# Four graph layers on one core: layer 1's projection by seven block products, its matrix divided before use, and its scores placed between layer 2's products

## The chip, the cores and the metric

The kernel runs on one core of a Trainium2 chip. The time is device microseconds of one launch, the median over several runs. The engines are named as in the profile: PE (TensorE, matrix products; PEld are its weight loads), DVE (VectorE), ACT (ScalarE), POOL (GpSimd) and SP (SyncE, whose queue issues nearly all DMA transfers here). Each engine works through its own list of instructions in order and waits on semaphores for the others.

## The reference, cut to what matters

`x` is 128 graphs of 64 nodes with 512 features, `adj` is 128 matrices of 64 x 64. Four layers follow each other, each wrapped as `x = layernorm(x + layer(x))`, all in float32. The change is in layer 1 and in the order of the steps around it:

```python
def _L1_gnn_ref(x, A_shape, w, a):
    y = x @ w
    s = y @ a
    A = s[..., :, None] + s[..., None, :]
    A = jnp.tanh(A / 8.0) * 8.0
    A = jnp.where(A >= 0, A, 0.1 * A)
    A = jnp.exp(A) * A_shape
    A = A / jnp.sum(A, axis=-1, keepdims=True)
    A = A * jnp.sum(A_shape, axis=-1, keepdims=True)
    return A @ x @ w
```

Layer 0 is a hypergraph convolution with a hidden width of 1024 (products with W1 and W2), layer 2 three graph convolutions (products with W1, W2, W3), layer 3 an attention with eight heads (products with the q, k and v parts of `W_qkv`, and with `W_out`), a mask and a bias.

## The kernel before

**Tiles.** The 8192 rows are cut into 16 groups of 512 rows: four pairs of graphs, 128 rows each. A group's state `xg` is a tile of 128 partitions x 4 pairs x 512 features in a pool of three buffers (`xp`), so the x load of a group waits until the store of the group three before it has landed. Features are brought to the partitions by `graph_T` (L341), which at the same time multiplies each graph by its 64 x 64 matrix: 64 small matmuls (128 passes in the trace) for each half of the pairs, copied out of PSUM by ACT into a `Left` (L367), the left side of a large product.

**Large products by seven.** All large products but layer 1's go through `multiply` (L409). It cuts left, right and result into 2 x 2 blocks and forms seven block products in place of eight, in the order B11, T1, T2, B21, T3, B22, T4. `product` (L391) issues one of them: four 128x256 matmuls, which float32 makes eight passes in the trace. The four sums of left blocks that this needs are made on DVE by `Left.sums` (L377). Of the weights, three blocks come from the input; the four differences T1 to T4 are formed once, in group 0, by `Weight.make` (L197), written to DRAM, and loaded from there for later groups. Three partial results are taken out of PSUM in the middle by `snap` (L414; ACT copies, or DVE adds where a residual is added) and added to later ones on DVE (L434, L436, L438). `multiply` is a generator: it yields once, after the third product, so that other work can be placed in its middle. Its accumulators `a`, `b`, `c` are the names of its PSUM tiles; with the key they make names such as `a_q` (first accumulator of the q product) or `c_wo`.

**Weights.** The class `Stream` (L244) walks a list of uses in the order of the schedule and issues weight loads on SP's queue, as long as at most 20 tiles of 256 KB are held (`RING`). Layer 1's `w` is a special case there: `None` in place of a `Weight`, four tiles of 128 rows x 512.

**Layer 1** is the end of `first_half` (L543). `s4` holds the scores of the rows (L611), `e` spreads them on a diagonal (L615), a matmul with `bones` (ones on two 64 x 64 blocks) gives `ss` (L619), and on it follow an add, Tanh, the leaky part, and Exp (L624 to L627). Then `tn = t * adn` (L630) has rows summed (L633) for a reciprocal `r` of each node's denominator, scaled by the row sums of `adj` (L635), and `t = t * atc` (L631) is the undivided matrix, transposed. `graph_T` applies it (step c3), and 16 matmuls of 512 columns (32 passes), in four PSUM tiles, multiply by `w` (L645). DVE multiplies each result by `r` and adds the residual in one instruction (L648); `layer_norm` (L328) ends the layer.

**Order.** The work of a group is in two generators: `first_half` (layers 0 and 1) and `second_half` (layers 2 and 3). A list written out by hand, `order` (L875), gives a step of the whole kernel: `a.` entries advance the first half of group s, `b.` the second half of group s-1, and `t.` the late part of the second half (from the v product on) of group s-2. 18 steps run it: step 0 has only `a`, steps 1 to 15 have an `a` part beside the others, 16 and 17 none. The list sets priorities. A planner then places every instruction on its engine's list when the kernel is built, by its own estimate of the times, so that work further down the list can stand ahead of an instruction that it expects to wait: in the trace a block product of `wo` stands among those of l2c although the list has it behind them. `tc.issue_after` (used by `behind`, L364) puts instructions behind a given one on its engine: behind the last DVE add of a product (`last_add`, L438).

**Layer 3's end.** `wo` is the product with `W_out`; it adds the residual `xg`, to which the bias `bo_bc` was added on DVE in step xT (L744). Then come the last norm and the store on SP's queue (L778), all within step `o`.

Of the kernel before, what the change touches and what calls it, by code (L numbers as in the profile page):

```python
# [20 lines left out]
T = G * P  # L21
KD = D // P
# [18 lines left out]
def kernel(  # L41
# [198 lines left out]
    w_g = [Weight(t, 0, f"gw{'abc'[n]}") for n, t in enumerate((gW1, gW2, gW3))]  # L240
    w_q, w_k, w_v = (Weight(Wqkv, n * D, f"w{'qkv'[n]}") for n in range(3))
    w_o = Weight(Wout, 0, "wo")

    class Stream:  # L244


        def __init__(self, uses):
            self.todo = []
            for wt, q in uses:
                if wt is None:  # L250
                    self.todo.append((wt, q, None, KD))
                elif q == 0:
                    self.todo.append((wt, q, None, 8 * wt.halves))
                else:
                    self.todo += [(wt, q, what, wt.halves) for what in ORDER]
            self.here = {}
            self.held = 0

        def pump(self):
            while self.todo and self.held + self.todo[0][3] <= RING:  # L260
                wt, q, what, n = self.todo.pop(0)
                if wt is None:
                    got = []
                    for c in range(KD):
                        t = wring.tile([P, D], FP, name=f"ww_{q}_{c}", tag="wq")
                        nc.sync.dma_start(out=t, in_=w[c * P : (c + 1) * P, :])
                        got.append(t)
                elif q == 0:
# [6 lines left out]
        def take(self, wt, q, what=None):  # L275
            self.pump()
            if wt is None:
                return self.here.pop((wt, q, None))
# [6 lines left out]
        def done(self, wt, q, what=None):  # L285

            if wt is None:
                self.held -= KD
            elif q > 0:
# [74 lines left out]
    def behind(key):  # L364
        return tc.issue_after(last_add[key]) if key in last_add else nullcontext()
# [40 lines left out]
                )  # L406
        stream.done(*wt_q, what)

    def multiply(lefts, wt_q, dst, key, flipped=False, res=None, before=None):  # L409


        acc = [ps_acc.tile([P, 2, Q], FP, name=f"{n}_{key}", tag="acc") for n in "ab"]
# [1 line left out]
        def snap(ps, m, n, what):  # L414
            t = work.tile([P, 2, Q], FP, name=f"{what}_{key}", tag="w")
            if res is None:
                nc.scalar.copy(t, ps)
            else:
                nc.vector.tensor_add(t, ps, res(m, n))  # L419
            return t  # L420
# [3 lines left out]
        if before is not None:  # L424
            before()
        s1 = snap(pa, 0, 0, "u1")
        product(pc, lefts, wt_q, T1, True, False, flipped)
        s5 = snap(pc, 1, 1, "u5")
        product(pa, lefts, wt_q, T2, False, False, flipped)
        s2 = snap(pa, 0, 1, "u2")  # L430
        yield
        pb = ps_acc.tile([P, 2, Q], FP, name=f"c_{key}", tag="acc")
        product(pb, lefts, wt_q, B21, True, True, flipped)
        nc.vector.tensor_add(dst(0, 0), pb, s1)  # L434
        product(pa, lefts, wt_q, T3, False, False, flipped)
        nc.vector.tensor_add(dst(1, 1), pa, s5)  # L436
        product(pc, lefts, wt_q, B22, False, True, flipped)
        last_add[key] = nc.vector.tensor_add(dst(0, 1), pc, s2).ins  # L438
        product(pa, lefts, wt_q, T4, False, True, flipped)
# [9 lines left out]
    def nat(t):  # L449

        return lambda m, n: t[:, 2 * m : 2 * m + 2, n * Q : (n + 1) * Q]
# [91 lines left out]
    def first_half(g):  # L543
# [90 lines left out]
        nc.vector.reciprocal(r, r)  # L634
# [6 lines left out]
        ww = stream.take(None, q)  # L641
        for p in range(G):
            ps = ps_acc.tile([P, D], FP, name=f"l1w_{q}_{p}", tag="acc")
            for c in range(KD):
                nc.tensor.matmul(  # L645
                    ps, left.t[:, c, p * P : (p + 1) * P], ww[c], start=(c == 0), stop=(c == KD - 1)
                )
            nc.vector.scalar_tensor_tensor(xg[:, p, :], ps, r[:, p : p + 1], xg[:, p, :], ALU.mult, ALU.add)  # L648
            if p == 1:
                yield "p1"  # L650
        stream.done(None, q)
        layer_norm(xg, f"l1_{q}")
        yield "p2"

# [6 lines left out]
    def second_half(g):  # L661
# [82 lines left out]
        nc.vector.tensor_add(xg, xg, bo_bc.unsqueeze(1).to_broadcast([P, G, D]))  # L744
# [33 lines left out]
        nc.sync.dma_start(  # L778
            out=out[q * T : (q + 1) * T, :].rearrange("(p t) d -> t p d", t=P), in_=xg
        )  # L780
        yield "o"

    def scores(g, duo, qT, kT):

# [66 lines left out]
    def attend(g, duo, pts, v, left):  # L851
# [29 lines left out]
    used = {  # L881
        "a.w1a": w_1[0], "a.w1b": w_1[1], "a.w2": w_2, "a.p2": None, "b.l2a": w_g[0], "b.l2b": w_g[1],
        "b.l2c": w_g[2], "b.q": w_q, "b.k": w_k, "t.v": w_v, "t.o": w_o,
    }
    lag = {"a": 0, "b": 1, "t": 2}
# [81 lines left out]
```

## Time and profile before

| | before |
|---|---|
| median of 4 runs | 2866.37 us (2865.38 to 2867.57) |
| the profiled execution's own time | 2865.38 us |
| its span, first to last instruction | 2863.6 us |
| mean granted PE clock | 0.992 |
| layer 1's product, PE busy (L645) | 229.2 us, 512 passes of 596 ns, overlapping |
| a block product's first form (`a_q`), PE busy | 85.3 us, 360 passes of 380 ns, overlapping |
| weight load of layer 1 (`ww`) | 64 transfers of 256 KB, 2.8 us to land |
| x load, store of the result | 6.0 us and 4.3 us to land (1024 KB each) |

How to read it: times are in microseconds, the mean of one instruction in ns. Matmul passes are pipelined, so the durations of passes that follow each other overlap; what a run of them takes is read from start to start in the timeline. A wait is listed by who waited and for what, with total, times and longest. The chain of waits follows back from the last instruction to what released it at each step; with a window it shows the part of the chain in that stretch. A row with a line number of a helper (L402 in `product`, L333 in `layer_norm`) covers all its callers, so tiles' names tell them apart.

### The profile page before, as it was taken

The numbers are of one execution on the slowest core, as the hardware profiler recorded it, in microseconds if no ns is written. First come the engines' busy times: TensorE is split into PE (matmuls) and PEld (weight loads), VectorE is DVE, ScalarE is ACT, GpSimd is POOL, SyncE is SP. The second block draws the span as 40 slices with busy tenths as digits, with TensorE's granted clock in tenths as the row PEclk, the third lists the DMA queues.
The fourth block names the chain that finished last, engine by engine and source line by source line (L and its number), as shares of the span: only waits on it lengthen the run. The fifth ranks groups of instructions, "written<-read, shape, count | busy, mean of one in ns | idle before, by whom it ended". The sixth has DMA issues, their size and how long they took to land.

```text
span 2863.6 us, 66482 instructions
## 1 busy us (share of the span) xinstructions
PE 2793.3 (98%) x28386; PEld 2284.6 (80%) x28386; DVE 1955.9 (68%) x3849; ACT 774.8 (27%) x1380; POOL 7.8 (0%) x17
## 2 busy tenths in 40 slices
PE   6899999999999999999999999999999999999998
PEld 4687878878788787887878788787887878888776
DVE  6667776667665766766667666776767677666655
ACT  2122322223222232322223222232232323122232
POOL 1000000000000000000000000000000000000000
PEclk9899999999999999999999999999999999999999
DMA  6444445444444445444444444444444444344431
GB/s 190 144 134 130 132 127 162 130 150 127 154 134 132 143 129 161 128 129 152 130 154 127 131 154 131 149 127 157 132 125 150 132 155 128 119 158 130 134 118 60
DMA packets 300294, 393.14 MB, mean 137 GB/s; under 512 B 57152, under 2 KB 172128, under 8 KB 300000
## 3 DMA queue, kind: packets, MB, share of 16 engines
q1 hardware_dynamic: 299344, 387.28, 43.6%
q8 instruction: 225, 3.69, 0.5%
q0 software_dynamic: 656, 1.60, 0.2%
q14 instruction: 69, 0.57, 0.1%
HBM read 358.90 MB, written 29.88 MB: 136 GB/s over the span
## 4 chain that ended last, share of the span: by engine, by line
PE 81%; DVE 14%; DMA 2%; ACT 2%; issue 1%; SPq 0%; DVEq 0%; ACTq 0%
PE a_l0w L402 15%; PE b_l0w L402 7%; PE a_l2b L402 4%; PE c_l0w L402 4%; PE a_l2a L402 4%; PE a_l2c L402 4%; PE a_k L402 4%; PE a_v L402 4%; DVE st_l L333 4%; PE a_q L402 3%; PE gt_l L351 3%; PE gt_l0h L351 2%; PE a_wo L402 2%; PE b_l2a L402 2%; PE b_v L402 2%; PE b_k L402 2%
## 5 line engine op out<-in xcount | busy, mean ns | idle before, releaser
L645 PE MATMUL l1w<-ww,aT_l 128*128 128x512 f32 x512 | 229.2, 596 | 0.0
L645 PEld LDWEIGHTS l1w<-ww,aT_l 128*128 128x128 f32 x512 | 96.1, 190 | 104.5 <-issue 97.6
L333 DVE BATCH_NORM_STATS2 st_l<-x 128x6 f32<-128x512 f32 x256 | 168.2, 679 | 1.7
L324 ACT ACTIVATE rs_l<-mv_l,eps_t 128x4 f32<-128x4 f32 x64 | 19.0, 297 | 546.7 <-DVE mv_l L334 546.7
L402 PE MATMUL a_l0w<-w2w,aT_l0h 128*128 128x256 f32 x720 | 164.3, 381 | 0.0
L402 PEld LDWEIGHTS a_l0w<-w2w,aT_l0h 128*128 128x128 f32 x720 | 135.6, 190 | 18.8
L568 ACT ACTIVATE h<-h 128x1024 f32<-128x1024 f32 x64 | 67.6, 1057 | 264.8 <-DVE h L438 241.4
L337 DVE TENSOR_SCALAR x<-x,mv_l,rs_l 128x512 f32<-128x512 f32 x256 | 122.1, 541 | 1.2
L359 ACT COPY aT_l<-gt_l 128x512 f32<-128x512 f32 x192 | 99.0, 599 | 58.0 <-PE gt_l L351 58.0
L402 PE MATMUL b_l0w<-w2w,s_l0h 128*128 128x256 f32 x480 | 108.5, 379 | 0.0
L402 PEld LDWEIGHTS b_l0w<-w2w,s_l0h 128*128 128x128 f32 x480 | 91.2, 190 | 12.4
L402 PE MATMUL a_l2b<-gwbw,aT_h 128*128 128x256 f32 x360 | 86.9, 384 | 4.7 <-ACT aT_oT L871 4.7
L703 ACT ACTIVATE aT_h<-gth,gb_col 128x256 f32<-128x256 f32 x128 | 48.4, 489 | 159.0 <-PE gth L695 159.0
L402 PE MATMUL a_l0w<-w1aw,aT_l 128*128 128x256 f32 x360 | 88.2, 388 | 0.0
L419 DVE TENSOR_TENSOR u_l0w<-a_l0w,b_bc 128x512 f32<-128x512 f32 x64 | 44.0, 687 | 64.4 <-PE a_l0w L402 64.4
L402 PE MATMUL a_l2c<-gwcw,aT_h 128*128 128x256 f32 x360 | 87.7, 386 | 0.0
L402 PE MATMUL a_l2a<-aT_l,gwaw 128*128 128x256 f32 x360 | 86.6, 383 | 1.0 <-ACT aT_l L359 1.0
L402 PE MATMUL a_l0w<-w1bw,aT_l 128*128 128x256 f32 x360 | 87.3, 379 | 0.0
L402 PE MATMUL a_v<-wvw,aT_xT 128*128 128x256 f32 x360 | 86.6, 383 | 0.0
L402 PE MATMUL a_wo<-wow,aT_oT 128*128 128x256 f32 x360 | 86.0, 382 | 0.2 <-DVE x L436 0.2
L507 DVE TENSOR_TENSOR smat<-sps,rb 64x256 f32<-64x256 f32 x32 | 13.5, 422 | 105.4 <-PE sps L504 104.9
L402 PE MATMUL a_q<-aT_xT,wqw 128*128 128x256 f32 x360 | 85.3, 380 | 0.2 <-ACT aT_xT L742 0.2
(427 smaller groups left out, 6119.9 us busy)
## 6 DMA issues: line engine op xcount, KB each, us to landing
w2w<-w2k SPq DMA_DIRECT2D x210, 256.0 KB, 2.6
x<-in_x_dram SPq DMA_DIRECT2D x16, 1024.0 KB, 6.0
ww<-in_w_dram SPq DMA_DIRECT2D x64, 256.0 KB, 2.8
out_dram<-x SPq DMA_DIRECT2D x16, 1024.0 KB, 4.3
w1aw<-w1ak SPq DMA_DIRECT2D x60, 256.0 KB, 2.7
w1bw<-w1bk SPq DMA_DIRECT2D x60, 256.0 KB, 2.6
gwaw<-gwak SPq DMA_DIRECT2D x60, 256.0 KB, 2.6
gwbw<-gwbk SPq DMA_DIRECT2D x60, 256.0 KB, 2.6
```

Source lines behind the costliest of these rows:

```text
L324: nc.scalar.activation(rs, mv[:, :, 1], AF.Sqrt, bias=eps_t)
L333: nc.vector.bn_stats(st, xg[:, p, :])
L337: nc.vector.tensor_scalar(xg[:, p, :], xg[:, p, :], mv[:, p, 0:1], rs[:, p : p + 1], ALU.subtract, ALU.mult)
L351: nc.tensor.matmul(ps[g][f * C : (f + 1) * C, c, p, :], src(2 * duo + p)[rows, c0 : c0 + C], mat[rows, 2 * duo + p, :], start=True, stop=True,
L359: nc.scalar.copy(o[:, :, :, g, :], ps[g])
L402: nc.tensor.matmul(acc[:, blk, :], lhsT, rhs, start=(first and blk == 0 and i == 0), stop=(last and i == n_k - 1), skip_group_check=True,)
L419: nc.vector.tensor_add(t, ps, res(m, n))
L507: nc.vector.tensor_mul(sm[rows], s_ps[h][rows], rb[rows])
L568: nc.scalar.activation(hn, hn, AF.Relu)
L645: nc.tensor.matmul(ps, left.t[:, c, p * P : (p + 1) * P], ww[c], start=(c == 0), stop=(c == KD - 1))
L703: nc.scalar.activation(o[:, :, h, :], ps[h][:, c].rearrange("p (d a) i -> p d (a i)", d=2), AF.Relu, bias=gb2_col[:, k : k + 1],)
```

## The change

- Layer 1's `w` becomes a `Weight` (`w_l1`), and its projection goes through `multiply`: seven loads for a group in place of four, four differences made and stored in group 0, left sums on DVE, a result tile `y` in SBUF. The special case leaves `Stream`.
- The matrix is divided before it is applied: `t` is multiplied by `atc` at once, a matmul with `bones` gives the column sums `den` of the transposed matrix in PSUM, DVE takes their reciprocal (`rd`, 128 x 256) and multiplies. `tn`, `r` and the reduction are gone. The last multiply-add takes `y` and the row sums of `adj`.
- `multiply` gets `stops`, the block products after which it yields. l2c yields after the third and the fifth, `ss` stands between the fifth and the end. `wo` yields after the first and the third, and `den` stands between these.
- The bias add of layer 3 moves from step xT behind the last add of the q product. The last norm and the store become a step of their own, `ln3`, behind `b.q`, issued behind the last add of the next group's q product.

```diff
+    w_l1 = Weight(w, 0, "w")
...
-    def multiply(lefts, wt_q, dst, key, flipped=False, res=None, before=None):
+    def multiply(lefts, wt_q, dst, key, flipped=False, res=None, before=None, stops=(3,)):
...
         s1 = snap(pa, 0, 0, "u1")
+        if 1 in stops:
+            yield
         product(pc, lefts, wt_q, T1, True, False, flipped)
...
         s2 = snap(pa, 0, 1, "u2")
-        yield
+        if 3 in stops:
+            yield
...
         nc.vector.tensor_add(dst(1, 1), pa, s5)
+        if 5 in stops:
+            yield
...
         nc.scalar.activation(t, t, AF.Exp, scale=8.0)
-
-        tn = grp.tile([P, G, C], FP, name=f"tn_{q}", tag="tn", bufs=1)
-        nc.vector.tensor_mul(tn, t, g["adn"])
         nc.vector.tensor_mul(t, t, g["atc"])
-        r = small.tile([P, G], FP, name=f"r_{q}", tag="r")
-        nc.vector.reduce_sum(r, tn, axis=AX.X)
-        nc.vector.reciprocal(r, r)
-        nc.vector.tensor_mul(r, r, g["rowsum"])
         yield "ss"
+
+        den = ps_gt.tile([P, G, C], FP, name=f"den_{q}", tag="gt")
+        nc.tensor.matmul(
+            den.rearrange("p a i -> p (a i)"), bones.rearrange("p g j -> p (g j)"),
+            t.rearrange("p a i -> p (a i)"), start=True, stop=True,
+        )
+        rd = grp.tile([P, G, C], FP, name=f"rd_{q}", tag="rd", bufs=1)
+        nc.vector.reciprocal(rd, den)
+        nc.vector.tensor_mul(t, t, rd)
+        yield "den"
         left = Left(f"l1_{q}")
         for duo in range(2):
             graph_T(pair, t, left.t, duo, f"l1_{q}")
+        left.sums()
         yield "c3"
...
+        y = big.tile([P, G, D], FP, name=f"y_{q}", tag="big")
+        for _ in multiply([left], (w_l1, q), nat(y), f"l1w_{q}"):
+            yield "p1"
         for p in range(G):
...
+            nc.vector.scalar_tensor_tensor(
+                xg[:, p, :], y[:, p, :], g["rowsum"][:, p : p + 1], xg[:, p, :], ALU.mult, ALU.add
+            )
         layer_norm(xg, f"l1_{q}")
...
-        for _ in multiply([h2], (w_g[2], q), nat(g3), f"l2c_{q}"):
-            yield "l2c1"
+        for n, _ in enumerate(multiply([h2], (w_g[2], q), nat(g3), f"l2c_{q}", stops=(3, 5))):
+            yield f"l2c{n + 1}"
...
-        nc.vector.tensor_add(xg, xg, bo_bc.unsqueeze(1).to_broadcast([P, G, D]))
         yield "xT"
...
+        with behind(f"q_{q}"):
+            nc.vector.tensor_add(xg, xg, bo_bc.unsqueeze(1).to_broadcast([P, G, D]))
         yield "q"
...
-        for _ in multiply([left], (w_o, q), nat(xg), f"wo_{q}", res=nat(xg)):
-            yield "o1"
-        layer_norm(xg, f"l3_{q}")
...
+        for n, _ in enumerate(multiply([left], (w_o, q), nat(xg), f"wo_{q}", res=nat(xg), stops=(1, 3))):
+            yield f"o{n + 1}"
         yield "o"
+        with behind(f"q_{q + 1}"):
+            layer_norm(xg, f"l3_{q}")
...
+        yield "ln3"
...
-        b.l2b1 a.c2a b.l2b a.c2b b.gb3 load a.w21 b.gh a.w2 b.l2c1 b.l2c a.ss t.o1 a.c3 b.agg t.o a.p1 b.xT
-        a.p2 b.q1 b.q b.k1 prep b.k b.dots
+        b.l2b1 a.c2a b.l2b a.c2b b.gb3 load a.w21 b.gh a.w2 b.l2c1 b.l2c2 a.ss b.l2c t.o1 a.den t.o2 a.c3 b.agg t.o a.p1 b.xT
+        a.p2 b.q1 b.q t.ln3 b.k1 prep b.k b.dots
```

More of the change, by code (lines that the diff above doesn't have):

```diff
@@ L249, in __init__ @@
             for wt, q in uses:
[L250 to L252 removed]
+                if q == 0:
                     self.todo.append((wt, q, None, 8 * wt.halves))
@@ L261, in pump @@
                 wt, q, what, n = self.todo.pop(0)
[L262 to L268, printed above, removed]
+                if q == 0:
                     got = wt.load_quads()
@@ L273, in pump, with take @@
                 self.held += n
-        def take(self, wt, q, what=None):
+        def take(self, wt, q, what):
             self.pump()
-            if wt is None:
-                return self.here.pop((wt, q, None))
             if q > 0:
@@ L283, in take, with done @@
             return self.here[wt, q][what]
[L285 to L289, printed above, removed]
+        def done(self, wt, q, what):
+            if q > 0:
                 self.held -= wt.halves
@@ L639, in first_half @@
             graph_T(pair, t, left.t, duo, f"l1_{q}")
+        left.sums()
         yield "c3"
-        ww = stream.take(None, q)
+        y = big.tile([P, G, D], FP, name=f"y_{q}", tag="big")
+        for _ in multiply([left], (w_l1, q), nat(y), f"l1w_{q}"):
+            yield "p1"
         for p in range(G):
[L643 to L651, printed above, removed]
+            nc.vector.scalar_tensor_tensor(
+                xg[:, p, :], y[:, p, :], g["rowsum"][:, p : p + 1], xg[:, p, :], ALU.mult, ALU.add
+            )
         layer_norm(xg, f"l1_{q}")
@@ L774, in second_half @@
         yield "osum"
-        for _ in multiply([left], (w_o, q), nat(xg), f"wo_{q}", res=nat(xg)):
-            yield "o1"
-        layer_norm(xg, f"l3_{q}")
-        nc.sync.dma_start(
-            out=out[q * T : (q + 1) * T, :].rearrange("(p t) d -> t p d", t=P), in_=xg
-        )
-        yield "o"
+        for n, _ in enumerate(multiply([left], (w_o, q), nat(xg), f"wo_{q}", res=nat(xg), stops=(1, 3))):
+            yield f"o{n + 1}"
+        yield "o"
+        with behind(f"q_{q + 1}"):
+            layer_norm(xg, f"l3_{q}")
+            nc.sync.dma_start(
+                out=out[q * T : (q + 1) * T, :].rearrange("(p t) d -> t p d", t=P), in_=xg
+            )
+        yield "ln3"
     def scores(g, duo, qT, kT):
@@ L881 @@
     used = {
-        "a.w1a": w_1[0], "a.w1b": w_1[1], "a.w2": w_2, "a.p2": None, "b.l2a": w_g[0], "b.l2b": w_g[1],
+        "a.w1a": w_1[0], "a.w1b": w_1[1], "a.w2": w_2, "a.p2": w_l1, "b.l2a": w_g[0], "b.l2b": w_g[1],
         "b.l2c": w_g[2], "b.q": w_q, "b.k": w_k, "t.v": w_v, "t.o": w_o,
```

## The prediction

> **What bounds the kernel.** First the page's top: the busy share of each engine. Then one steady step as a window (from one start of the q product to the next, 173.19 us), and the waits of TensorE (PE) over the steady stretch.
>
> ```profile
> PE 2793.3 (98%) x28386; PEld 2284.6 (80%) x28386; DVE 1955.9 (68%) x3849; ACT 774.8 (27%) x1380; POOL 7.8 (0%) x17
> ```
> ```profile
> 1300.68:1473.87 173.19, 172.72 (x1774) 141.36 (x1773) 119.54 (x237) 48.12 (x86) 0.00 (x0) 1.00 0.46 140
> ```
> ```profile
> PE a_l2b L402 <- ACT aT_oT L871: 4.7, 14, 0.3
> PE a_q L402 <- ACT u_q L417: 0.6, 3, 0.2
> ```
>
> PE works 172.7 of 173.19 us, at full granted clock (1.00); between 300 and 2680 us it waits 5.3 us in all. So PE work taken out of a step shortens it, as long as nothing else becomes late. Fifteen steps (1 to 15) are like this; step 0 is a bare chain of group 0, and steps 16 and 17 have no layer 1.
>
> But one place in the step is close to a second bound. The chain of waits leaves PE there and runs through DVE for 26 us, up to the third q product (columns: start, length, piece):
>
> ```profile
> 1450.94 0.41 DVE rowsum L472
> ...
> 1460.54 1.81 DVE x L337 x4
> ...
> 1468.41 2.20 DVE x L744
> ...
> 1476.62 0.19 DVE mv_l L334
> 1476.86 0.18 issue
> 1477.04 0.57 ACT u_q L417
> 1477.66 1.99 PE a_q L402 x8
> ```
>
> DVE has no gap from 1450.7 to 1476.8 us. The change works just there, so DVE's sum must be made as well as PE's.
>
> **PE's sum.** Before, the projection is 32 matmuls of 512 columns; a product of `multiply` is 8 of 256. From the timeline (start, span of the run, count at the end):
>
> ```profile
> 1460.51 5.31 PE L645 MATMUL l1w<-ww,aT_l 128*128 128x512 f32 x12
> 1465.76 1.21 PE L737 MATMUL xtp<-identc,x 64*128 64x64 f32 x32
> 1466.90 7.13 PE L645 MATMUL l1w<-ww,aT_l 128*128 128x512 f32 x16
> ```
> ```profile
> 1309.72 1.89 PE L402 MATMUL b_q<-s_xT,wqw 128*128 128x256 f32 x8
> 1311.45 1.89 PE L402 MATMUL a_q<-aT_xT,wqw 128*128 128x256 f32 x8
> 1313.18 1.89 PE L402 MATMUL a_k<-aT_xT,wkw 128*128 128x256 f32 x8
> ```
>
> Start to start: 12 take 5.25 us, 16 take 6.97 (the next run starts at 1473.87), the first 4 took 1.71: 13.93 us, 435 ns each. A product takes 1.73 us, 216 ns a matmul, seven 12.09. That removes 1.84 us a step. It adds `den`, two passes of a 128x256 matmul with `bones`, the same form as `ss`, which started at 1443.47 with its successor at 1443.90: 0.43 us; `rbps` took 0.52. I take 0.45. Net **-1.39 us a step**.
>
> The Trainium skill, "TensorE: Matmul & The Clock Gate", section "Back-to-back issue gap", speaks against this: it gives sustained 81 ns a matmul at 128 columns and 131 at 512, so narrow matmuls cost more per column. Its straight line gives about 98 ns at 256 (an estimate); scaled to the 435 ns here, 56 matmuls would take 18.2 us and each step grow by 4.3 us, some 68 us in all. The rows above differ: 216 is half of 435, so the sum goes by the rows.
>
> **DVE's sum.** Between `ss` and the third q product DVE loses: `tn` 0.43, its row sum 0.41, the small reciprocal 0.18 and product 0.16 (L630, L633 to L635), about 1.2; layer 3's norm, four bn_stats at 0.6 of pitch, aggregates, reciprocal and four L337 (1.8), about 4.9; the bias add L744, 2.2. Together 8.3. It gains: four sums of `left.sums()`, 2.5 (four such sums start at 1519.65, and what follows them at 1522.19); three adds out of PSUM at 0.6 each, 1.8; one 128x256 multiply, 0.42; and `rd`, a reciprocal of 128x256 out of PSUM that no row shows. Its nearest rows (minimum/median/maximum ns) are:
>
> ```profile
> L634 DVE RECIPROCAL r<-r x16: 178/178/179, 116.8 to 2661.4; 128x4 f32<-128x4 f32 x16
> L826 DVE RECIPROCAL sum<-sum x64: 184/203/204, 294.5 to 2834.6; 128x8 f32<-128x8 f32 x64
> ```
>
> Four more elements cost 25 ns, 6.3 ns each; a 128x2 one takes 162 ns, which makes 6.8. From below 0.42 us, as any other 128x256 row (L631); from above 178 ns and 252 elements at 7 ns, 1.94 us. I take 1.9, since the rows that are reciprocals set the slope. "VectorE: DVE Perf Modes", section "First, the fixed hardware budget", has the reciprocal run an iterative divide with a repeat count of 8; at its 0.96 GHz eight cycles an element would be 2.1 us (an estimate), 0.2 more than mine.
>
> Gained 6.6, lost 8.3: DVE's stretch shrinks by 1.7 us, PE's by 1.4. It stays close, and is not worse. The chain also entered DVE through the load of the next adn, which `tn` had held back until 1447.8; without `tn` that load and its readers come earlier. The four final multiply-adds (L648) stay at 0.73, their input in SBUF; the all-SBUF row L657 of that form has 0.75. ACT gets four 0.58 copies (three snapshots, one result): 2.3 us on an engine busy 48 of 173.
>
> **The waits that it adds.** (1) `ss` to layer 1's graph product. Before: `ss` 1443.47, graph product 1448.75. Now the softmax-like chain (5.2 us) is followed by den 0.45, rd 1.9, multiply 0.42 and about 0.2 for each hand-over. `ss` is two products earlier (3.5 us), and the last two products of l2c, then the first of wo, lie between it and `den`: 5.2 us; wo's next two between `den` and the graph product: 3.5 against 2.9. Covered with up to 0.6 to spare; without that cover it costs 2.9. (2) `left.sums()` before layer 1's second product, which also needs a fourth accumulator bank, freed by wo's first add: agg (2.4 us) and the rest of wo lie between. (3) The sums and rd stand in DVE's queue ahead of agg's adds and the norm of layer 2, which the transposes (xtp) wait for; three products instead of 16 matmuls come before xtp: 5.2 us against 7.0. From the graph product's end DVE needs the copies 1.2, sums 2.5, agg's adds 2.5, statistics 2.8, wo's adds 2, root 0.5, first norms 1: 12.5. PE has agg 2.4, three products of wo 5.2 and three of layer 1 5.2: 12.8. This is the tightest; I book 0.15 us a step. (4) On ACT the new snapshots queue with the norms' square roots, which wait for DVE; one in the wrong order holds PE's third product (q pays 0.1 to 0.2 now).
>
> (5) The store of layer 3 moves, and on SP's queue the load of the next x waits for it, because x has three buffers:
>
> ```profile
> 1467.78 0.38 SPq L778 DMA_DIRECT2D out_dram<-x  x1
> 1472.02 0.37 SPq L119 DMA_DIRECT2D x<-in_x_dram  x1
> ```
>
> From q's start (1473.87): q's last add ends at 11.7 us; then bias add 2.3, norm 5.3 with its square root, so the store at 19.3, landed 4.3 later; x issued at 23.7, landed 6.0 later: 29.7. Its first reader, the layer 0 graph product, starts 33.3 after q (1334.00 against 1300.68). Slack 3.6 us, 29 before. Weight loads behind the store lose nothing: they run some 40 us ahead (w1a issued 1477.5, used 1518). DVE is idle from 1485.6 to 1492.9 and nothing else waits for the two moved pieces (the bias add's reader is wo, a step later), so they cost nothing there; without the idle time they would come back as 7 us of DVE. Weights: seven loads of 256 KB for four, 2.7 us to land, on queues busy 44%: hidden.
>
> **Step 0 and the end.** In step 0 the chain is bare: before, `t` was done at 116.4, graph product 116.54, projection 120.17 to 134.56. Now `t` 0.5 earlier, then den 1.2 (ss took that cold), rd, multiply and hand-overs: graph product at about 119.9, +3.3; a wait of 0.8 for the first sums; the projection 2.3 shorter; four subtractions of new weights and the result copy, up to 1; group 1's products fill part. I take +1. In step 16 the norm and bias add leave the way of q (waits of 0.3 and 0.25 there): -0.5.
>
> **Sum.** 15 x (-1.39 + 0.15) + 1 - 0.5 = -18.1 us on the profiled run's 2865.4 (span 2863.6 and 1.8 around it): 2847.3. The median shown is 1.0 higher: 2848.3, so **2848**.
>
> **Rivals.**
> 1. The DVE or ACT order of waits (3) and (4) takes back part. For it: the chain above already runs through DVE. Against it: DVE's sum shrinks. A square root ahead of a snapshot, or xtp late, at 0.9 us a step costs 13.5: 2861; between 0.4 and 1.3 us, 2854 to 2867.
> 2. No gain: DVE's stretch keeps its length, so the step does. 2866.
> 3. Slower: the x load comes late at the layer 0 graph product. It decides once layer 3's norm and x end 3.6 us later than above; each us beyond costs 13 (13 of the 16 x loads wait on a semaphore), so past 5.0 us the change loses. One number for it: x's slowest landing was 12.9 instead of 6.0; that is 3.3 late, 43 us: 2891. Against it: typical landings are 5.4 to 6.0, and four v products can go first.
> 4. More gain: no new wait, step 0 loses nothing, small gaps close: -1.6 a step, 2841 or less.
>
> **Chances.** Forecast 0.62 (2842 to 2854), rival 1 0.20, rival 2 0.05, rival 3 0.07, rival 4 0.06. The range 2838 to 2864 leaves out rival 3, rival 2, and the ends of 1 and 4. A measurement can tell 0.2%, 5.7 us: faster is below 2860.6. That takes the forecast, rival 4 and 0.12 of rival 1: 0.80. Same: the rest of rival 1 and rival 2, 0.13. Slower: 0.07.
>
> **What would show it.** PE busy falls by some 22 us (16 x 1.39) and the step to about 171.9. `den` shows 0.4 to 0.5 us, `rd` 1.7 to 2.2. PE's waits in the steady stretch stay under 8 us; above 20 with xtp, a_q or the layer 1 product as the waiter is rival 1. PE waiting in the layer 0 graph product for DMA x is rival 3. Wrong from the root would be a product of layer 1 above 1.73 us.

## The result and the profile after

The changed kernel takes 2870.5 us (median of 41 runs, 2867.9 to 2874.6) against 2867.0 for the kernel before (61 runs, 2864.8 to 2869.2): a ratio of 1.0013, 95% interval 1.0008 to 1.0017. That is within the 0.2% that was called "no difference", a little on the slow side, and 22.5 us above the forecast. The profiled execution has a span of 2870.3 us against 2863.6, and its own time is 2872.0.

First the same three readings as before: the top of the page, one steady step from a start of the q product to the next, and PE's waits between 300 and 2680 us.

```profile
PE 2776.2 (97%) x28802; PEld 2363.6 (82%) x28802; DVE 2043.4 (71%) x3933; ACT 811.3 (28%) x1444; POOL 7.8 (0%) x17
```
```profile
1140.45:1313.09 172.64, 171.50 (x1799) 146.19 (x1798) 124.97 (x242) 50.36 (x90) 0.00 (x0) 1.00 0.47 144
```
```profile
PE a_wo L391 <- DVE x L428: 8.8, 13, 0.7
PE a_l2b L391 <- ACT aT_oT L869: 4.7, 14, 0.3
```

PE's busy time fell by 17 us, and the step did get shorter, but by about half a microsecond and not by 1.24. A waiter is new: the last block product of `wo`, up to 0.7 us in each of 13 steps. And since 15 shorter steps cannot make a longer span, something outside them must have lost more. The starts of the first product of layer 0 (`a_l0w` with `w1aw`), one in each step, cut the span into pieces:

| piece | before | after | difference | forecast |
|---|---|---|---|---|
| up to group 0's first product | 20.09 | 19.98 | -0.11 | 0 |
| step 0 | 122.96 | 138.34 | **+15.38** | +1 |
| step 1 | 162.58 | 162.92 | +0.34 | -1.24 |
| steps 2 to 14, thirteen of them | 2251.88 | 2244.95 | **-6.93** (-0.53 each) | -16.1 (-1.24 each) |
| step 15 and the end | 306.09 | 304.11 | -1.98 | -1.74 |
| span | 2863.6 | 2870.3 | +6.7 | -18.1 |

Of the 24.8 us between forecast and result, 14.4 lie in step 0, 1.6 in step 1 and 9.2 in the steady steps. The last piece is right only in sum, by luck: by the starts of the q products step 15 gained 0.5 instead of 1.24, and the rest 1.4 instead of 0.5.

**The steady step.** The timeline of PE where `wo` and layer 1 meet, and the chain of waits over the same stretch, in the changed kernel:

```profile
1294.87 1.89 PE L391 MATMUL b_wo<-wow,s_oT 128*128 128x256 f32 x8
1296.60 1.89 PE L391 MATMUL a_l1w<-ww,aT_l 128*128 128x256 f32 x8
1299.18 1.99 PE L391 MATMUL a_wo<-wow,aT_oT 128*128 128x256 f32 x8 [0.69 <-DVE x L428]
...
1309.26 1.89 PE L391 MATMUL b_l1w<-ww,s_l 128*128 128x256 f32 x8
1311.26 1.99 PE L391 MATMUL a_l1w<-ww,aT_l 128*128 128x256 f32 x8
```
```profile
1292.90 2.40 DVE x L719 x4
1295.29 1.19 DVE st_l L322 x2
...
1298.55 0.59 DVE x L428
...
1310.61 0.61 DVE y L428
```

A block product that waits for nothing follows the one before it after 1.73 us. `wo`'s last (`a_wo`) starts 2.58 after its predecessor, 0.85 too late (0.64 in one of the 13 steps); layer 1's last (the second `a_l1w`) 2.00 after, about 0.28 too late. Both wait for a DVE add that empties their bank (L428, the add after T3). The chain shows why the adds are late: in DVE's list `wo`'s two adds stand behind the adds of the aggregation (L719) and the statistics of layer 2's norm (L322); layer 1's stand behind the sums for q. The wait list has the first at 0.7 and the second not at all, because the profile lets a product last 1.89 us although the next can start after 1.73: the pitch from start to start is the safer reading.

All terms of a step, by such pitches: layer 1's product 13.93 us as 32 passes is 7 x 1.73 = 12.1 as block products (-1.84); `den` +0.43; the late starts +0.85 and +0.28; +0.20 because these two late products take 1.83 instead of 1.73 to their successor's start; +0.19 for the products on either side of the transposes (1.82 and 1.83); -0.40 for q, whose third product started 0.30 late before and took 1.83; -0.28 for l2c, whose last product before was late as well (12.14 instead of 12.42 us in all); and +0.03 around `ss`. The sum is -0.54, and the two windows differ by -0.55 (172.64 against 173.19).

**Step 0.** PE's waits up to group 1's first product, before and after, and DVE ahead of the product with W2, after and (last line) before:

```profile
PE wa_ps L310 <- DVE rs_l L325: 4.5, 1, 4.5
...
PE bwps L232 <- issue: 3.5, 1, 3.5
...
PE gt_l L351 <- DVE smat L507: 1.3, 1, 1.3
```
```profile
PE bwps L232 <- issue: 9.2, 1, 9.2
PE wa_ps L299 <- DVE wa_diag L297: 8.3, 1, 8.3
...
PE gt_l L340 <- DVE smat L501: 5.2, 2, 4.6
```
```profile
67.88 0.42 DVE L459 TENSOR_TENSOR hn<-hn,wb 128x256 f32<-128x256 f32 x1 [5.95 <-DMA wb<-in_adj_dram]
...
69.46 0.68 DVE L370 TENSOR_TENSOR s_l0h<-aT_l0h 128x512 f32<-128x512 f32 x1
```
```profile
65.23 0.69 DVE L381 TENSOR_TENSOR s_l0h<-aT_l0h 128x512 f32<-128x512 f32 x1
```

`hn` at L459 belongs to the preparation of a later group. It waits 5.95 us for its load at the head of DVE's list, and behind it stand the left sums that group 0's own product with W2 needs: they start at 69.46 instead of 65.23, and W2's first product at 83.19 instead of 77.83. Followed down the step, the delay is 5.4 us there, 9.3 at `wa_ps`, 9.6 at `ss`, 12.8 at layer 1's graph product and 15.3 at group 1's first product. So some 5.4 us arise up to W2, 3.8 between W2's end and `wa_ps`, 3.15 in the chain from `ss` to the graph product, and 2.5 behind it.

### The profile page after: what moved, and what is told of

It reads as the page before. It is cut to its first block, busy times and chain, and to the rows that moved or that the text cites. A ratio compares the mean times of both kernels' runs of the same rounds, so it can differ in the third digit from the quotient of the medians.

```text
span 2870.3 us, 67654 instructions
## 1 busy us (share of the span) xinstructions
PE 2776.2 (97%) x28802; PEld 2363.6 (82%) x28802; DVE 2043.4 (71%) x3933; ACT 811.3 (28%) x1444; POOL 7.8 (0%) x17
## 4 chain that ended last, share of the span: by engine, by line
PE 80%; DVE 8%; ACT 3%; issue 0%; DVEq 0%; ACTq 0%
PE a_l0w L391 14%; PE b_l0w L391 7%; PE a_v L391 4%; PE a_k L391 4%; PE a_l2b L391 4%; PE a_l2c L391 4%; PE a_q L391 4%; PE a_l2a L391 4%; PE c_l0w L391 4%; PE a_wo L391 3%; PE gt_l L340 3%; PE gt_l0h L340 2%; PE a_l1w L391 2%; PE b_v L391 2%; PE b_k L391 2%; PE b_l2c L391 2%
## 5 line engine op out<-in xcount | busy, mean ns | idle before, releaser
L322 DVE BATCH_NORM_STATS2 st_l<-x 128x6 f32<-128x512 f32 x256 | 165.3, 673 | 0.6
L391 PEld LDWEIGHTS a_l0w<-w2w,aT_l0h 128*128 128x128 f32 x720 | 135.6, 190 | 18.8
L391 PE MATMUL a_l1w<-ww,aT_l 128*128 128x256 f32 x360 | 86.9, 384 | 1.7
L391 PEld LDWEIGHTS a_wo<-wow,aT_oT 128*128 128x128 f32 x360 | 67.1, 190 | 23.2 <-DVE x L428 14.2
L391 PE MATMUL a_k<-aT_xT,wkw 128*128 128x256 f32 x360 | 85.0, 379 | 0.0
```

The source lines that it names most:

```text
L322: nc.vector.bn_stats(st, xg[:, p, :])
L391: nc.tensor.matmul(acc[:, blk, :], lhsT, rhs, start=(first and blk == 0 and i == 0), stop=(last and i == n_k - 1), skip_group_check=True,)
```

## The experiments

Theory: (A) step 0 loses because `tn` was the late reader of `adn`; without it the buffers of `adn` come free early, the planner puts later groups' preparation ahead on DVE, and a load holds the whole list. (B) The steady step loses to DVE's order, at two adds. Rivals: step 0 loses to the longer chain and the new weights alone; and the steady step loses to what block products really cost, or to DVE's sheer length. All kernels start from before or from after. The table has the results; "usual step" is the pitch of most of the steps 2 to 14.

| kernel | median us (runs) | ratio to before, 95% | steps 0 and 1 | usual step |
|---|---|---|---|---|
| before | 2867.0 (61) | 1 | 285.5 | 173.19 |
| after | 2870.5 (41) | 1.0013 [1.0008, 1.0017] | 301.3 | 172.65 |
| rowsum_late | 2863.6 (11) | 0.9985 [0.9976, 0.9994] | 290.9 | 172.64 |
| free_adn | 2891.8 (4) | 1.0089 [1.0073, 1.0104] | 300.2 | 173.2 to 175.6 |
| prep_behind | 2861.5 (11) | 0.9980 [0.9972, 0.9989] | 291.8 | 172.64 |
| seven_only | 2869.0 (10) | 1.0003 [0.9994, 1.0012] | 284.3 | 173.5 |
| den_only | 2874.0 (10) | 1.0024 [1.0014, 1.0033] | 294.0 | 173.33 |
| order_only | 2862.5 (10) | 0.9985 [0.9976, 0.9994] | 288.9 | 172.83 |
| agg_last | 2874.2 (11) | 1.0023 [1.0015, 1.0032] | 300.9 | 172.33 |
| ln_act | 2871.1 (11) | 1.0013 [1.0005, 1.0022] | 297.5 | 172.64 |
| split_agg | 2858.5 (6) | 0.9969 [0.9957, 0.9981] | 291.7 | 172.33 |
| step0 | 2859.1 (6) | 0.9968 [0.9956, 0.9979] | 284.7 | 172.64 |
| best | 2855.8 (5) | 0.9959 [0.9947, 0.9972] | 286.0 | 172.33 |
| order_step0 | 2857.0 (5) | 0.9965 [0.9953, 0.9978] | 283.6 | 172.83 |
| xs | 2848.6 (4) | 0.9934 [0.9921, 0.9948] | 287.8 | 171.95 |
| t3 | 2850.4 (4) | 0.9941 [0.9928, 0.9955] | 286.6 | 171.86 |
| t3xs | 2849.6 (5) | 0.9937 [0.9924, 0.9951] | 288.2 | 171.86 |

### Step 0: who frees adn

**rowsum_late** (from after): the row sums of `adn` are taken behind `t * atc`, so that `adn` has a late reader again.

```diff
         nc.vector.tensor_mul(t, t, g["atc"])
+        with tc.issue_after(ins):
+            nc.vector.reduce_sum(rowsum, g["adn"], axis=AX.X)
```

> The changed kernel with one edit: the row sums of adj are taken right behind t * atc, where tn stood, so that adn has its late reader back. Theory A (step 0 lost 5.6 us because adn, free at once, let the preparation of later groups stand far ahead in DVE's list, and DVE then waited 6 us in order for the load of wb in front of the sums for w2): the first w2 product of group 0 starts near 77.8 us instead of 83.2, group 1's first layer 0 product near 152.7 instead of 158.3, the time falls by 5 to 6 us to about 2865. Rival B (step 0 is late because of the added DVE work and weights, and the early preparation only fills idle time): w2 stays near 83, the time near 2870.

Measured: W2's first product starts at 73.61 instead of 83.19, and steps 0 and 1 lose 10.3 of the 15.7 us that they had gained in length. W2 even starts earlier than before the change (77.83). The usual step is unchanged, but six are 0.1 to 1.5 us longer; in five places DVE's `hn` waits up to 1.6 us for the load of `adn`, which now comes later.

**free_adn** (from before): the reverse. The multiply before the row sum reads `t` twice, so nothing late reads `adn` (the row sums, and so the results, are then others).

```diff
-        nc.vector.tensor_mul(tn, t, g["adn"])
+        nc.vector.tensor_mul(tn, t, t)
```

> The kernel before, with tn = t * t in place of t * adn (the row sums are then of another matrix; same instructions), so that adn has no late reader. Theory A: step 0 grows as in the changed kernel, w2 starts near 83 instead of 77.8, the time is 4 to 6 us longer than before, about 2872. Rival B: within 1 us of before, 2867.

Measured: one operand changed, no instruction more or less, and the kernel is 0.9% slower: steps 0 and 1 are 14.7 us longer, the steady steps up to 2.4 (there `wo`'s last product waits up to 2.1). The wait of `bwps`, 3.5 before and 9.2 after, is longer still:

```profile
PE bwps L232 <- issue: 11.9, 1, 11.9
```

So a reader of `adn` that seemed to be pure cost, and that the forecast booked as 1.2 us less DVE work, held the planner back. This is (A) by itself, without seven products and without `den`.

**prep_behind** (from after): `adn` stays free, but the DVE part of a group's preparation is issued behind the last add of layer 1's product two groups earlier.

```diff
     def prepare(g):
+        with behind(f"l1w_{g['q'] - 2}"):
+            prepare_body(g)
+
+    def prepare_body(g):
```

> The changed kernel with DVE's part of a group's preparation issued behind the last add of layer 1's product two groups earlier. Theory A (far-ahead preparation cost step 0 its w2): step 0 as with the late row sums (128.8 us between the first layer 0 products of groups 0 and 1, against 138.3), and, since no adn load is tied to the score chain now, every steady step at 172.65 where the late row sums had some of 173 to 174: time 2861. Rival B (the early preparation was useful, and its delay comes back at rbps): steps of 173 or more, 2866 or longer.

Measured: steps 0 and 1 take 291.8, 9.4 less than after, and the steady steps 172.64, but for one of 173.08: nearly the same gain as from the late reader, without its longer steps. Two ways of keeping the preparation back give nearly the same; that settles (A) for some 9 to 10 us of the 15.7.

### The parts alone

**seven_only** (from before): only the projection through `multiply`, with `r` as the factor and the old order.

```diff
+        left.sums()
...
-        ww = stream.take(None, q)
...
+        for _ in multiply([left], (w_l1, q), nat(y), f"l1w_{q}"):
+            yield "p1"
```

> The kernel before with only the projection by seven products (division as before, by r; order as before). Theory C (in the steady step the block products are worth their 1.84 us on PE, less some 0.9 us of waits of wo's and layer 1's last products for DVE adds; step 0 loses some 6 us by the weights' differences, the loads behind them and the norm that now starts only at the projection's end): step 172.2, step 0 longer by 6, time about 2858. Rival D (DVE's stretch has no room, the products bring nothing): step 173.2, time 2867 to 2875.

Measured: the usual step is 0.3 us longer than before, though PE has 1.84 less to do, for a wait that the prediction named under (2), layer 1's second product for the bank that `wo`'s first add empties:

```profile
PE b_l1w L403 <- DVE x L435: 20.1, 14, 1.7
```

The first two steps take 284.3 against 285.5, but that is a balance. W2's product starts at 71.77, 6.1 us earlier than before; 3.4 are lost again between its end and `wa_ps`, which waits 7.9 for `wa_diag` (8.3 in the changed kernel), and 2.3 behind the graph product, where `smat` holds PE for 4.6 instead of 1.3. So the part with the new weights and the residual at the end does cost step 0 some 5 to 6 us; that rival is wrong only as the whole cause. That the weights alone delay `wa_ps` is not shown: free_adn has no new weights and loses 3.6 in the same place.

**den_only** (from before): only the division by `den`, with the row sums held late as in rowsum_late, and 16 wide matmuls.

```diff
-        nc.vector.reciprocal(r, r)
...
+        nc.vector.reciprocal(rd, den)
+        nc.vector.tensor_mul(t, t, rd)
...
-        a.ss t.o1 a.c3
+        a.ss t.o1 a.den a.c3
```

> The kernel before with only the division by den (16 matmuls of 512 columns as before, order as before but den behind wo's third product, row sums kept behind t * atc so that adn has its late reader). Theory F (den costs its 0.43 us on PE in each step and its chain of 3.2 us once, in step 0; rd's 1.76 us on DVE is partly on the path, since DVE's stretch is full): step 173.6 to 174.5, time 2877 to 2890. Rival G (tn, its sum and r, 1.2 us of DVE, leave the stretch and pay for it): step 173.2, time 2868 to 2871.

Measured: 0.14 us more a step (`den` takes 0.54 here, and q's third product no longer waits, -0.41), and 8.4 us more in steps 0 and 1. Of these, 3.15 are the longer chain before the graph product, 1.9 lie before W2's start, 0.5 behind the graph product and 2.8 in step 1; what causes those 1.9 and 2.8 stays open.

**order_only** (from before): only the moves (`ss` inside l2c, the stops of `wo`, bias add and last norm moved).

> The kernel before with only the moves: scores inside l2c, the stops of wo, layer 3's bias add and norm behind the q products (no den; projection and division as before). Theory C (DVE's stretch from wo to q is the second bound; these moves take 7 us of DVE out of it, but PE has no less work): steps lose at most the 0.3 us that q waits, 172.8 to 173.0, step 0 unchanged, time 2863 to 2866. Rival H (what the moves put behind q is late there: the x load or k's adds): steps of 173.5 or more, time above 2870.

Measured: 0.36 us less a step: q is 0.41 and l2c 0.28 shorter, as in the changed kernel, and `wo` 0.31 longer, since its last product starts 0.21 late. The moves alone make the kernel 0.15% faster than before, which is clear of the scatter, though under the 0.2% that was called "no difference". In the steady step the three parts alone sum to about +0.1 us, and together they give -0.54: seven products need the new order, since it puts `wo`'s first add ahead of layer 1's second product.

### The steady step: order or length

**agg_last** (from after): in the list, layer 2's whole aggregation goes behind `wo`.

```diff
-        ... a.c3 b.agg t.o a.p1 b.xT
+        ... a.c3 t.o b.agg a.p1 b.xT
```

> The changed kernel with the rest of wo listed ahead of layer 2's aggregation (order: a.c3 t.o b.agg a.p1). Theory C (what the steady step lost is PE's wait for the adds of wo and layer 1, which stand in DVE's list behind the sums and the aggregation's adds and statistics): the waits of wo's last product go, the step falls from 172.65 to about 171.9, the time by some 11 us to about 2859. Rival E (DVE is full there, so the wait moves on to xtp, the sums for q or layer 1's last product): step 172.5 to 173, time 2868 to 2875.

Measured: `wo`'s wait is gone and the step is 0.32 shorter, but two smaller waits take its place, and the end of the kernel loses 6 us (step 16 waits 5.7 us for the norm):

```profile
PE a_l1w L391 <- DVE y L428: 5.0, 13, 0.4
...
PE xtp L732 <- DVE x L326: 2.7, 13, 0.2
```

**ln_act** (from after): the four last passes of layer 2's norm (1.9 us) go from DVE to ACT.

```diff
-        layer_norm(xg, f"l2_{q}")
+        layer_norm(xg, f"l2_{q}", act=True)
```

> The changed kernel with the last pass of layer 2's norm, four 0.5 us instructions, on ACT in place of DVE (one small DVE instruction more). Theory C (the length of DVE's work between wo and q binds): the waits of wo's last product stay, as they come before it, but those of layer 1's last product go and the transposes come in time: step 172.65 to about 172.3, time about 2865. Rival I (order, not length: DVE had 5 us without work between that norm and the sums for q): no change, step 172.6, time 2869 to 2871.

Measured: 1.9 us of DVE work less in the tight stretch, and the usual step stays as it was (172.64). So the length of DVE's work between `wo`'s adds and q does not hold the step; in the changed kernel DVE even stands idle for 5 us before the sums for q, from 1302.4 to 1307.4. This run cannot speak for `wo`'s last product, since the four passes stand behind its adds; for that product it is agg_last, with the same work in another order, that shows the order.

**split_agg** (prep_behind, and): the aggregation yields between its adds and its norm, and `wo`'s rest comes between them.

```diff
+        yield "add"
         layer_norm(xg, f"l2_{q}")
...
-        ... a.c3 b.agg t.o a.p1 b.xT
+        ... a.c3 b.add t.o b.agg a.p1 b.xT
```

> The changed kernel with two edits: the preparation of later groups waits on DVE behind the last add of layer 1's product two groups earlier (as in the run that had this alone: 2861.5 us, steps of 172.64), and layer 2's aggregation yields between its two adds and its norm, with the wo product's rest between them in the list. Theory: a steady step loses 0.64 us of wo's last product waiting for DVE, because wo's third product's add stands in DVE's list behind the norm's statistics; with the adds of wo ahead of the statistics that wait goes (8.7 us over the steady stretch to under 3) and the step falls from 172.64 to 172.0 to 172.2, the whole to 2852 to 2855. Rival: the wait only moves, to layer 1's first product or to the transposes behind it, as when the whole aggregation was put last (5.0 and 2.7 us there): step 172.4 to 172.6, whole 2858 to 2861.

Measured: the step falls to 172.33, less than hoped. The start of `wo`'s last product is still 0.54 late, since its adds still stand behind layer 1's four sums and the adds of the aggregation.

### All repairs

**step0** (prep_behind, and): `make_wa`, the product of `w` and `a` that the scores need, is called earlier, so that its loads of `w` are not behind the stores of the new differences on SP's queue; and group 1's preparation is placed ahead of layer 1's projection. The text on record calls the first of these differences of layer 0's weights, which is wrong; the edit is this one:

```diff
+        if q == 0:
+            make_wa()
         yield "w21"
...
+            if step == 0 and what == "a.p1":
+                prepare(groups[1])
```

**best** is step0 with split_agg. **order_step0** is order_only with these two edits of step 0.

> The changed kernel with only step 0 repaired: the preparation behind layer 1's product two groups earlier, the differences of layer 0's first weights formed earlier (behind the second product's first part, before the wait for W2), and group 1's preparation placed ahead of layer 1's projection in step 0. The order of the steady step is that of the changed kernel. Theory: of the 15.3 us that step 0 lost, all but the 3.2 of the longer chain before layer 1's graph product come back: step 0 from 138.3 (130.0 with the first edit alone) to 123 to 125, the steady step stays 172.64, the whole 2854 to 2857. Rival: step 0 is held by the load of the weights on SP's queue whatever DVE does: step 0 stays at 128 to 130, whole 2860 to 2862.

> Both of the former together: the split aggregation and the three edits to step 0. Theory: they touch different stretches and so add up: steps of 172.0 to 172.2, step 0 of 123 to 125, whole 2845 to 2849, which is the forecast of 2848 reached by taking away the two waits that it left out. Rival: they share DVE and one undoes the other: 2852 or more.

> The kernel before with only the moves in the order (scores inside layer 2's last product, wo's two stops, bias add and last norm moved), with 16 wide matmuls and the old division kept, and with the two edits to step 0. It tells what seven products and the division by column sums are worth when the rest is as good as it gets. Theory: its step stays at 172.83, as with the moves alone (2862.5 us, step 0 of 125.6); step 0 gains 1 to 3: 2859 to 2862, so the seven products with the division are worth about 12 us (0.8 a step times 15) in the kernel that has all repairs. Rival: the moves do it all, and the kernel with all repairs is not faster than this one by more than 4 us.

Measured: step 0 alone falls further than expected, to 117 us, but step 1 gives 6 back (167.8 instead of 161.8), so only their sum tells: 284.7, 7.1 less than with prep_behind, and 0.8 less than before. So the whole loss of 15.7 can be undone, though not each piece of it by its own cause: the same two edits also gain 5.3 in order_only (288.9 to 283.6), which has no seven products. The profiled execution of step0 was at 2856.3, the median at 2859.1. For best the gains did not fully add up: 2855.8, where 2845 to 2849 was expected: its step is 172.33 and not 172.0, four of the 13 are 0.2 to 1.8 longer still, and steps 0 and 1 take 286.0. And order_step0, with the old projection and division, is just 1.2 us behind best. Up to here, seven products were worth almost nothing even in a repaired kernel.

What was left by pitch in best was 0.64 at `wo`'s last product (0.54 late, 0.10 behind it), 0.38 at layer 1's last and 0.19 beside the transposes. Three more kernels tell whether these are waits or the price of block products.

**xs** (best, and): the sums for q become a step of their own, behind layer 1's fifth product.

```diff
-        left.sums()
         yield "xT"
+        left.sums()
+        yield "xs"
...
-        ... b.agg a.p1 b.xT
+        ... b.agg a.p1 b.xT a.p1b b.xs
```

> The kernel with all repairs so far (split aggregation, three edits to step 0: 2855.8 us, steps of 172.33) with one more: layer 3's left sums become a step of their own behind layer 1's fifth product, so that on DVE layer 1's adds are no longer all behind them. Theory: start to start, layer 1's last product is late by 0.28 us because its bank's add stands behind the four sums, and a product that had to wait starts its first pass 0.10 slower; both go: step 171.95, whole 2850 to 2851. Rival: the 0.28 are no wait for DVE but what a product costs behind the transposes: step 172.33.

Measured: the step is 171.95 and the median 2848.6. Layer 1's last products, start to start:

```profile
1464.26 1.89 PE L391 MATMUL b_l1w<-ww,s_l 128*128 128x256 f32 x8
1465.99 1.89 PE L391 MATMUL a_l1w<-ww,aT_l 128*128 128x256 f32 x8
1467.72 1.46 PE L391 MATMUL a_q<-aT_xT,wqw 128*128 128x256 f32 x6
```

1.73 and 1.73, where after had 2.00 and 1.83. It was a wait for DVE's order, and both its parts, 0.28 and 0.10, went with it.

**t3** (best, and): two of layer 1's four sums, and layer 2's norm, are issued behind the add of `wo`'s T3. **t3xs** has both edits.

```diff
+            with behind(key):
+                nc.vector.tensor_sub(s3, self.quad(0, 0), s3)
+                nc.vector.tensor_sub(s4, self.quad(0, 1), s2)
...
+        with behind(("T3", f"wo_{q - 1}")):
+            layer_norm(xg, f"l2_{q}")
```

> The kernel with all repairs so far with another: two of layer 1's four left sums and layer 2's whole norm are issued on DVE behind the add of wo's third combination, so that wo's last product finds its bank free. Theory: the 0.41 us of wait and the 0.10 behind it go: step 171.82, whole 2848 to 2849. Rival: the norm, pushed back by some 1.5 us, is now late for the transposes: step 172.2 or more, whole 2853 or more, with the transposes as the waiter.

> Both of these edits. Theory: the step is PE's sum and nothing else: 173.19 before, less 1.84, plus 0.43 for den, less 0.44 for the wait of the q products that went, and 0.1 to 0.2 for products behind transposes: 171.4 to 171.5, whole 2842 to 2845, which is below the forecast of 2848. Rival: one of the waits moves on to the transposes or the graph product: 171.8 or more, whole 2848 or more.

Measured: in t3xs no block product of `wo` or layer 1 is late any more, but the norm, pushed back, now is: the transposes take 1.70 instead of 1.14 us.

```profile
1451.10 1.89 PE L392 MATMUL b_wo<-wow,s_oT 128*128 128x256 f32 x8
1452.82 1.89 PE L392 MATMUL a_wo<-wow,aT_oT 128*128 128x256 f32 x8
...
1459.82 0.94 PE L740 MATMUL xtp<-identc,x 64*128 64x64 f32 x18
1460.94 0.65 PE L740 MATMUL xtp<-identc,x 64*128 64x64 f32 x14 [0.18 <-DVE x L326]
```

So the rival held: 171.86 and not 171.4, the wait moved on by 0.56. In t3 alone layer 1's last product is on time as well, so the two edits do not add. Neither can be told from xs by its median. Against order_step0 with its wide matmuls, xs is 8.4 us faster: that is what seven products and `den` bring once most of their waits are gone (order_step0 has none of the later edits to the steady step, so a part may belong to these). What is shown is that each of the late products is a wait: `wo`'s last and layer 1's last both run at 1.73 in t3xs. With the transposes' 0.56 taken off, its step would be 171.3, 1.9 below before; no kernel run here reached it.

## Why the prediction was wrong

Point by point, in the prediction's own steps.

**PE's sum: right but for 0.19.** A block product takes 1.73 us in layer 1 too, `den` 0.43 (0.45 was taken): net -1.41 a step. Only the two products beside the transposes take 1.82 and 1.83.

**DVE's sum: right, and beside the point.** The reciprocal was taken at 1.9 us between 0.42 and 1.94:

```profile
L631 DVE RECIPROCAL rd<-den x16: 1757/1757/1759, 126.9 to 2665.3; 128x256 f32<-128x256 f32 x16
```

1.76 us. The other estimate, 2.1, read the repeat count of 8 that the Trainium skill gives for the reciprocal ("VectorE: DVE Perf Modes", section "First, the fixed hardware budget") as eight cycles an element; this run has 6.9 ns an element with all overhead in it, and does not agree. DVE's work in a whole step grew from 119.5 to 125.0 us, which is what the terms give when the 7.1 us that were only moved are left out (6.6 - 1.2 = 5.4), and in the stretch DVE has 5 us to spare.

**Waits (2) and (3), "I book 0.15 us a step": the first failed step.** The two waits that the prediction named did not come: layer 1's second product and the transposes start on time, so the sum under (3), 12.5 against 12.8, came out right. But it compared DVE's *total* up to the transposes with PE's. DVE works in order, and inside that total stood two adds that PE needs long before its end: they cost 0.85 and 0.28 of late start and 0.20 behind these. With the 0.19 beside the transposes that is 1.52 us a step where 0.15 was booked. On the other side, 0.68 was not booked either: q's third product and l2c's last one no longer start late, which order_only shows to come from the moves (the wait list, from which the prediction took "0.1 to 0.2" for q, understates 0.40 by pitch). So the step lost 0.54 and not 1.24. Not the total but the position of each add in the list had to be compared with the moment at which its bank is needed. This is the mechanism of rival 1, and its net price, 0.70 a step, lies in that rival's range of 0.4 to 1.3; the places are partly others, since it spoke of roots, snapshots and transposes. By itself this loss would have given about 2859, as rival 1 had it (2854 to 2867).

**Wait (1): right.** In the steady stretch layer 1's graph product appears in no wait. **Wait (4): right**, the root at 1298.58 stands in front of the snapshot at 1298.79 without holding it.

**Wait (5): right, with less room than reckoned.**

```profile
1509.93 0.38 SPq L119 DMA_DIRECT2D x<-in_x_dram  x1
```

The x load is issued 24.0 us after q's start at 1485.94 (23.7 was forecast), the store before it 18.8 after (19.3). The load lands 5.7 us later and is read at 1518.85: 3.2 us of slack, where 3.6 was reckoned. But landings vary more than the prediction's "typical landings are 5.4 to 6.0": over the 13 steady loads they took 5.4 to 8.1 us before and 5.7 to 7.8 after, and the slack was 1.3 to 3.3. No wait for it appears, so rival 3 did not come; at the nearest it was 1.3 us away.

**Step 0, "I take +1": the second failed step, and the larger.** It measured +15.4. The chain's +3.3 was right (3.15). What was left out is that removing an operation also removes its *read*. The prediction saw it, for the steady step ("without `tn` that load and its readers come earlier"), as a gain. It did not ask where the planner would put those earlier readers in the bare step 0, where no other group's work covers a DVE that waits 5.95 us for a load. Nor did it count `make_wa`'s loads behind the new stores on SP's queue (3.8 us up to `wa_ps`), or that the residual with the row sums comes at once at the end of seven products, so that `smat` of group 1 stands behind four multiply-adds and the statistics (wait of 4.6 instead of 1.3). The first is shown by free_adn, rowsum_late and prep_behind. The places of the other two are shown, since seven_only loses there too, without `den` and without the moves; their causes are read from the trace and were only tested together (step0).

**The signs.** PE's busy time fell by 17 us, not 22: the sign itself is blunt, since a late product's predecessor counts as busy for part of the wait. PE's listed waits came to 13.5 us, under the 20 that were to mean rival 1, and 4.7 of these were there before; pitches show 14.5 us of late starts at the two products in the same 13 steps. `den` and `rd` lie where they were said to.

## What to carry to other kernels

When an operation is removed, ask what its reads and waits held back, and where a planner will put the work that they release: one changed operand cost this kernel 0.9%. A faster product on the bounding engine brings its gain only as far as the small operations that free its banks stand early enough in the other engine's list; compare each one's place with its due time, never the sums of two engines. And cut a long kernel's span by one event in each step before explaining anything: the first step and the steady steps here went opposite ways.

## What the runs showed of the hardware that was not expected

A block product that had to wait, or that follows the 64-column transposes, takes 1.83 us to its successor's start and not 1.73; in xs and t3, the 0.10 vanished together with the wait. Narrow float32 passes cost no more per column than wide ones: 216 ns at 256 columns against 435 at 512, also in layer 1. In several of the repaired kernels one step that ends near 1330 to 1345 us is 0.2 to 1.8 us longer than its neighbours; in best and t3xs the graph product of the next group waits 1.6 us there for nothing that the profile shows. The cause stays open.
